# A local-attention stage with its first scores brought forward, its first softmax in halves, and a new order for the last tile

## The chip, the cores and the metric

The kernel runs on one core of one Trainium2 chip. The metric is device time in microseconds from the start to the end of the one program, taken as the median of several runs. All times in the profile are microseconds from the first instruction of one profiled execution.

## The reference

The reference is a small model of four residual layers on 4096 tokens (2 batches of 2048) of width 256: causal linear attention, a mixture of experts, local attention, and the same mixture of experts again. The change touches the third layer alone.

```python
windows = [max(4, 256 // 2**h) for h in range(16)]           # 256 128 64 32 16 8 4 4 ...
qk = layernorm(x) @ Wqk + bqk;  q, k = split(qk);  v = k
mask = (j <= i) & (j > i - windows[h])
att = softmax(where(mask, q @ k.T / 4, -inf));  out = att @ v  # 16 heads of 16
gates = softmax(layernorm(x) @ Wgate + bgate)                  # one per head
x = x + (out * gates) @ Wproj + bproj
# then, in the fourth layer
probs = softmax(layernorm(x) @ gate_w.T)                       # 8 experts
# threshold routing with a capacity per expert over all 4096 tokens, then two matmuls per expert
```

Six heads have windows of 256 down to 8; ten heads have a window of 4, and for them a token needs its own key and those of the three tokens before it.

## The kernel before

The 4096 tokens are 32 tiles of 128. Four tiles make a group (`GT = 4`), there are eight groups (`NG = 8`), four to a batch. Names of a group's tiles are 0 to 3.

The local-attention stage handles the two kinds of heads apart. The ten narrow heads are computed **by token**, with tokens on the partitions and without TensorE: `by_token` projects a tile on TensorE and VectorE adds the bias and puts the result into `tk` (L968); `shifts` copies the keys by one, two and three tokens into `ks` with small DMAs on SyncE's queue (L999 to L1004); `multiply` forms query times key (`pr`, L1044 and L1045); `sum_scores` sums over the 16 dimensions (`s4`, L1049); `softmax_begin` and `softmax_end` are the softmax over four scores, with the gate multiplied in; `weigh_values` multiplies the values (`pv`, on GpSimd, L1075 and L1078) and `sum_values` sums them (`og`, L1084). The six wide heads are computed **by channel**: `by_channel` projects a whole group with channels on the partitions (`qm`, `kT`); a `Tile` then does `scores` on TensorE, `maxima` on VectorE, `exponentials` on ScalarE, `transpose` (three PSUM tiles of 3, 4 and 2 blocks, for head 0, for heads 1 to 3, and for heads 4 and 5), `coefficients` (`cb`), `others` (the transposes `c_ps` of `og` and `cb`), `values` (`wo_ps`), and `project` (`pj_ps`, added to `x`). `Group.add_bias` adds the output bias to `x` on GpSimd (L955), `gates_begin` and `gates_end` are the gate's softmax, `values` builds the value tiles `wvm` and `wvb`.

When a tile's `x` is final, `finished` measures its mean and variance for the router. The router of a group, `Route`, does `normalize`, `transposes`, `logits`, `probabilities`, `normalized` (which writes `probs` and sends the rows to `rows_b` by DMA), `pairs` and `ranks` (which write `score`). The last group has two routes of two tiles each, `tails[0]` and `tails[1]`. After the last, the experts' first step reads all scores and loads its constants `cst_sel` by a DMA from GpSimd's queue.

The order of the instructions on TensorE, ScalarE, VectorE and GpSimd is written out by hand: inside `tc.manual_schedule(engines=ORDERED)` each engine issues in the order in which the program calls. SyncE's DMAs are placed by the scheduler. The opening brings group 0 up to its scores by token and group 1 up to its transposes; then `slot(g, i, now, last)` runs once for each tile, doing the second half of the tile before it (`last`), the first half of its own (`now`), and one quarter of the preparation of the next group (`coming`), of the norm of the one after (`behind`) and of the router of the one before (`past`). A tail of calls follows the last slot. The PSUM pool `mm` has four buffers, which all of these share. The opening and the loop before:

```python
own.transposes(None); own.keys_before()
for i in range(GT):
    own.by_token(i)
    if i % 2: own.shifts(i - 1, i + 1)
own.values()
for m in range(2): own.by_channel(m)
own.gates_begin(); own.gates_end(); own.add_bias()
measure(groups, 1, *range(GT)); then.norm.scale()
then.normalize(range(GT)); then.transposes()
for i in range(GT):
    own.multiply(i, nc.vector); own.sum_scores(i)
then.add_bias()
```

Of the kernel before, what the change touches and what calls it, by code (L numbers as in the profile page):

```python
# [16 lines left out]
P = 128  # L17
# [3 lines left out]
GT = 4  # L21
# [101 lines left out]
def hybrid_kernel(ctx: ExitStack, tc: tile.TileContext, x, wq, wk, wv, wo, wqk, bqk, wgate, bgate, wproj, bproj,  # L123
# [788 lines left out]
    def windowed_attention(src, added, route):  # L912
        src_t = src[0:N, :].rearrange("(g n p) d -> g p n d", p=P, n=GT)
        with ExitStack() as st:
# [22 lines left out]
            class Group:  # L937
# [84 lines left out]
                def gates_begin(self):  # L1022
                    self.gl = gl = pool.tile([P, GT, H], F32, name="gl", tag="gl")
                    gm = pool.tile([P, GT], F32, name="gm", tag="gm")
                    logits = self.tk[:, :, D4 + D : TOK]
                    nc.vector.reduce_max(gm, logits, axis=AX.X)
                    nc.vector.tensor_tensor(gl, logits, gm.unsqueeze(2).to_broadcast([P, GT, H]), ALU.subtract)
                    nc.scalar.activation(gl, gl, AF.Exp)

                def gates_end(self):  # L1030
                    gl = self.gl
                    gs = pool.tile([P, GT], F32, name="gs", tag="gs")
                    nc.vector.reduce_sum(gs, gl, axis=AX.X)
                    nc.vector.reciprocal(gs, gs)
                    nc.vector.tensor_tensor(gl, gl, gs.unsqueeze(2).to_broadcast([P, GT, H]), ALU.mult)
# [16 lines left out]
                def softmax_begin(self):  # L1052
                    s4 = self.s4
                    if self.first:
                        s4e = s4[:, 0, 1:NW, :].rearrange("p w h -> p (w h)")
                        nc.vector.tensor_tensor(s4e, s4e, con("shift"), ALU.add)
                    self.m4 = m4 = pool.tile([P, GT, NH4], F32, name="m4", tag="m4")
                    nc.vector.reduce_max(m4, s4.rearrange("p i w h -> p i h w"), axis=AX.X)
                    nc.vector.tensor_tensor(s4, s4, m4.unsqueeze(2).to_broadcast([P, GT, NW, NH4]), ALU.subtract)
                    nc.scalar.activation(s4, s4, AF.Exp, scale=0.25)  # L1060

                def softmax_end(self):

                    s4, m4 = self.s4, self.m4
                    nc.vector.reduce_sum(m4, s4.rearrange("p i w h -> p i h w"), axis=AX.X)
                    nc.vector.reciprocal(m4, m4)
                    nc.vector.tensor_tensor(m4, m4, self.gl[:, :, H4:H], ALU.mult)
                    nc.vector.tensor_tensor(s4, s4, m4.unsqueeze(2).to_broadcast([P, GT, NW, NH4]), ALU.mult)
                    self.og = pool.tile([P, GT, D4], F32, name="og", tag="og")
                    self.pvs = {}  # L1070

                def weigh_values(self, i):
                    s4 = self.s4
                    self.pvs[i] = pv = pool.tile([P, D4, NW], F32, name="pv4", tag="pr4", bufs=4)
                    nc.gpsimd.tensor_tensor(pv[:, :, 0].rearrange("p (h d) -> p h d", d=HD),  # L1075
                                            s4[:, i, 0, :].unsqueeze(2).to_broadcast([P, NH4, HD]),
                                            self.own[:, i, :].rearrange("p (h d) -> p h d", d=HD), ALU.mult)
                    nc.gpsimd.tensor_tensor(  # L1078
# [7 lines left out]
            class Tile:  # L1086


                def __init__(self, g, i):
                    self.g, self.i, self.t = g, i, (g % BG) * GT + i  # L1090

# [55 lines left out]
                def transpose(self, k):  # L1147
# [7 lines left out]
                    nc.scalar.copy(pt[:, skip:w, :], ps[:, skip:w, :])  # L1155
                    if k == 0:
                        self.pts = []
                    self.pts.append(pt)
# [79 lines left out]
            def slot(g, i, now, last):  # L1238
# [3 lines left out]
                if last:  # L1242
# [3 lines left out]
                    call(groups, last.g, "sum_values", last.i)  # L1246
                if i == 0 and g:
                    call(groups, g, "softmax_begin")
                if now:
# [4 lines left out]
                if now:  # L1254
                    now.maxima()
                    now.exponentials((2, 3))
                if i == 0 and not g:
                    now.exponentials((4, 5, 1, 0))
                    groups[0].softmax_begin()

                if i == 0:
                    call(groups, coming, "keys_before")
                    call(groups, g, "softmax_end")
# [10 lines left out]
                else:  # L1274
# [4 lines left out]
                    if g == NG - 1:  # L1279
# [153 lines left out]
```

## Time and profile before

| what | value |
|---|---|
| median of 3 runs | 940.69 us (940.29 to 940.84) |
| the profiled execution: its own time | 943.79 us |
| its span, first to last instruction | 941.7 us |
| mean granted TensorE clock | 0.906 |
| busy, share of the span | PE 80%, PE weight loads 53%, DVE 67%, ACT 40%, POOL 46% |
| 464.2 to 506.7 us, opening of local attention | PE 31.4, DVE 24.8, ACT 12.6, POOL 13.7 us busy of 42.5; clock 0.72 |
| 506.7 to 762.8 us, its tiles | PE 248.1, DVE 218.3, ACT 165.6, POOL 137.4 us busy of 256.1; clock 1.00 |
| 762.8 to 793.4 us, last tile and router | PE 16.1, DVE 19.7, ACT 8.3, POOL 5.4 us busy of 30.6; clock 0.75 |

In the profile PE is TensorE (PEld its weight loads), DVE VectorE, ACT ScalarE, POOL GpSimd, SPq the DMA queue that SyncE issues. A row gives the start, the duration, the engine, the line of the kernel, the operation, and output and input by the program's names; a bracket at the end gives how long the engine had been idle and what ended that. Idle time matters where its engine is the one that the rest waits for. The lines in the profile of before are those of the kernel before; in the changed kernel they stand a few lines lower.

### The profile page before, as it was taken

Reading aid. Unit: us, or ns where it says so; the run is one execution under the profiler, and the core shown is the slowest. Engines: PE = TensorE matmul, PEld = TensorE weight load, DVE = VectorE, ACT = ScalarE, POOL = GpSimd, SP = SyncE. Lnnn points to the kernel's source line nnn. Section 1 sums busy time; section 2 is a strip of 40 time slices with the busy share of each in tenths; the row PEclk is TensorE's granted clock in tenths of the full one; section 3 lists DMA queues with packets and bytes.
Section 4 is the critical chain, followed back from the end, with each engine's and each line's share of the span. In section 5 each row is a group of like instructions: output and inputs, shape, how many; then the busy total and the mean of one; then the engine's idle time right before and its main releaser. Section 6 shows DMA issues by size and latency. Waiting matters only on the chain. (4 is left out here: it accounts for less than half of the span.)

```text
span 941.7 us, 17226 instructions
## 1 busy us (share of the span) xinstructions
PE 755.1 (80%) x6422; PEld 494.6 (53%) x6422; DVE 627.8 (67%) x1670; ACT 380.3 (40%) x1075; POOL 436.7 (46%) x482
## 2 busy tenths in 40 slices
PE   6799999999998217877569999999999982168774
PEld 3576676676676114544335666665666661145442
DVE  4577778778677775532247878988988876755421
ACT  3444454544543122211124576675676661221110
POOL 2133334334234007888522644664655431058885
PEclk9799999999999557999778999999999995569997
DMA  9910101101102103455552123123132111025554
GB/s 317 264 36 24 47 2 47 47 2 47 46 20 74 31 0 81 76 83 83 111 152 59 41 58 95 33 81 94 30 89 84 57 46 41 1 70 74 80 81 60
DMA packets 64236, 65.08 MB, mean 69 GB/s; under 512 B 7084, under 2 KB 60825, under 8 KB 64153
## 3 DMA queue, kind: packets, MB, share of 16 engines
q1 hardware_dynamic: 50057, 44.00, 15.2%
q0 software_dynamic: 12720, 18.10, 11.8%
q10 hardware_dynamic: 1376, 1.90, 0.6%
q8 instruction: 50, 0.82, 0.4%
q14 instruction: 33, 0.27, 0.1%
HBM read 26.56 MB, written 27.56 MB: 57 GB/s over the span
## 5 line engine op out<-in xcount | busy, mean ns | idle before, releaser
L210 POOL TENSOR_TENSOR ln_rstd<-ln_rstd,cst_parts 128x4 f32<-128x4 f32 (+1 forms) x34 | 34.2, 1006 | 126.3 <-DVE ln_rstd L209 72.3
L235 ACT COPY xnT<-xnT_ps 128x512 f32<-128x512 f32 (+1 forms) x71 | 39.1, 579 | 127.0 <-PE xnT_ps L231 127.0
L883 PE MATMUL h_ps<-xnT,w_sb 128*128 128x512 f32 x128 | 67.8, 676 | 5.3 <-ACT xnT L235 3.5
L413 POOL TENSOR_TENSOR a_sb<-a_raw,cst_first 128x512 f32<-128x512 f32 x32 | 40.9, 1279 | 63.2 <-ACT a_raw L412 63.2
L896 DVE TENSOR_SCALAR y<-y_ps,xe 128x256 f32<-128x256 f32 x64 | 30.9, 484 | 51.8 <-PE y_ps L893 47.4
L893 PE MATMUL y_ps<-w_sb,hT 128*128 128x256 f32 x256 | 61.3, 386 | 4.6 <-DVE row L839 1.7
L415 DVE TENSOR_TENSOR a_sb<-s_ps,cst_first 128x512 f32<-128x512 f32 x96 | 60.0, 680 | 6.8 <-PE s_ps L401 6.8
L897 POOL DMA_INDIRECT out_rows<-y,idx x32 | 53.0, 1656 | 15.0 <-issue 7.3
L897 POOL DMA_INDIRECT mid<-y,idx x32 | 53.0, 1657 | 14.1 <-issue 7.9
L205 DVE BATCH_NORM_STATS2 ln_stats<-x 128x6 f32<-128x256 f32 x128 | 53.4, 418 | 8.5 <-DMA x<-in_x 4.4
L1155 ACT COPY pt<-pt_ps 128x256 f32<-128x256 f32 (+3 forms) x96 | 43.0, 469 | 38.8 <-PE pt_ps L1153 38.3
L966 PE MATMUL tk_ps<-wt_sb,xnT 128*128 128x432 f32 x128 | 56.2, 570 | 0.2 <-ACT xnT L235 0.2
L893 PEld LDWEIGHTS y_ps<-w_sb,hT 128*128 128x128 f32 x256 | 45.5, 189 | 18.2 <-ACT hT L885 3.9
L1144 ACT ACTIVATE wpr<-sn_ps,negm 128x128 f32<-128x128 f32 x128 | 45.9, 375 | 5.3 <-DVE negm L1130 5.3
L233 DVE COPY xnT<-xnT_ps 128x512 f32<-128x512 f32 (+1 forms) x29 | 19.0, 655 | 41.5 <-PE xnT_ps L231 41.4
L883 PEld LDWEIGHTS h_ps<-xnT,w_sb 128*128 128x128 f32 x128 | 26.2, 217 | 37.5 <-issue 25.8
L1153 PE MATMUL pt_ps<-cst_parts,wpr 128*128 128x128 f32 x280 | 44.0, 282 | 1.9 <-ACT wpr L1144 1.7
L1153 PEld LDWEIGHTS pt_ps<-cst_parts,wpr 128*128 128x128 f32 x280 | 30.8, 140 | 25.2 <-issue 6.9
L859 POOL DMA_INDIRECT xe<-rows_a,idx x32 | 33.7, 1054 | 20.9 <-DVE olo L812 11.7
L222 ACT ACTIVATE xr<-x,ln_shift,ln_rstd 128x256 f32<-128x256 f32 x56 | 29.1, 591 | 33.2 <-DVE ln_shift L220 18.6
L859 POOL DMA_INDIRECT xe<-rows_b,idx x32 | 32.7, 1023 | 20.9 <-DVE olo L812 11.4
L885 ACT ACTIVATE hT<-h_ps 128x512 f32<-128x512 f32 x32 | 19.1, 597 | 57.4 <-PE h_ps L883 56.2
(237 smaller groups left out, 2074.1 us busy)
## 6 DMA issues: line engine op xcount, KB each, us to landing
ks<-tk SPq DMA_DIRECT2D x21, 280.0 KB
rows_a<-xr SPq DMA_DIRECT2D x7, 528.0 KB
rows_b<-xr SPq DMA_DIRECT2D x7, 528.0 KB
x<-in_x SPq DMA_DIRECT2D x7, 512.0 KB
mid<-x SPq DMA_DIRECT2D x7, 512.0 KB
x<-mid SPq DMA_DIRECT2D x7, 512.0 KB
out_rows<-x SPq DMA_DIRECT2D x7, 512.0 KB
w_sb<-in_w1t SPq DMA_DIRECT2D x1, 2048.0 KB
```

What stands on the lines that cost most here:

```text
L205: nc.vector.bn_stats(self.stats[:, i, :], self.xin[:, i, :])
L235: nc.scalar.copy(xnT[:, c, :], pt)
L413: nc.gpsimd.tensor_tensor(a, raw, causal, ALU.mult)
L415: nc.vector.tensor_tensor(a, s_ps[j], causal, ALU.mult)
L859: read = nc.gpsimd.indirect_dma_start(out=xes[e][:, b, :], out_offset=None, in_=rows[:, :], in_offset=bass.IndirectOffsetOnAxis(ap=idx[e][ ...
L883: nc.tensor.matmul(h_ps, w1_sb[:, e, c, f * P : (f + 1) * P], xT[:, c, :], start=(c == 0), stop=(c == NC - 1))
L893: nc.tensor.matmul(y_ps, hT[:, f, b * P : (b + 1) * P], w2_sb[:, e, f, :], start=(f == 0), stop=(f == F // P - 1))
L897: add = nc.gpsimd.indirect_dma_start(out=acc[:, :], out_offset=bass.IndirectOffsetOnAxis(ap=idx[e][:, b : b + 1], axis=0), in_=y, in_offse ...
L966: nc.tensor.matmul(ps, self.xnT[:, c, i * P : (i + 1) * P], wt_sb[:, c, :], start=(c == 0), stop=(c == NC - 1))
L1144: nc.scalar.activation(self.pr[:, o : o + w], src, AF.Exp, bias=self.negm[:, h : h + 1], accum_out=self.den[:, h : h + 1])
L1153: nc.tensor.transpose(ps[:, n, :], self.pr[:, (o + n) * P : (o + n + 1) * P], ident)
L1155: nc.scalar.copy(pt[:, skip:w, :], ps[:, skip:w, :])
```

## The change

The opening and the end are put in another order, and several steps learn to work on part of a group or on another engine.

- `gates_begin`, `gates_end`, `softmax_begin` and `softmax_end` take a range of tiles. The opening calls each twice, for tiles 0 and 1 and for tiles 2 and 3; all later groups call them for four tiles as before.
- In the opening `by_channel` comes ahead of `by_token`; the first tile's `scores`, `maxima` and `exponentials` come in the midst of the `by_token` calls and no longer in `slot(0, 0)`; group 1 is measured, normalized and transposed earlier; `multiply` of tiles 1 and 3 goes from VectorE to GpSimd, `weigh_values` of tile 0 from GpSimd to VectorE. `add_bias` of group 0 comes after the products, `add_bias` of group 1 after `slot(0, 1)`.
- The last tile has no slot of its own. Its `sum_values` comes before its last exponentials; its three transposes run in the order of its heads' exponentials, (4, 5), (1, 2, 3), (0), the first two of them copied by VectorE; `tails[0]` is normalized and transposed after the last tile's `others`; both tiles of `tails[1]` are normalized on VectorE; the router of group 6 (`before`) does its last steps among these.

The built program has the same DMAs. On SyncE's queue the first group's 18 shift copies are issued in another order: the small ones (L1002) of each half first, which read the tile before, and then the six large ones (L999, L1000), where it had them in turn.

```diff
-                def gates_begin(self):
-                    self.gl = gl = pool.tile([P, GT, H], F32, name="gl", tag="gl")
+                def gates_begin(self, a=0, z=GT):
+                    if a == 0:
+                        self.gl = pool.tile([P, GT, H], F32, name="gl", tag="gl")
+                    gl, n = self.gl[:, a:z], z - a
...
-                def weigh_values(self, i):
+                def weigh_values(self, i, engine=nc.gpsimd):
...
-                def transpose(self, k):
+                def transpose(self, k, engine=None):
...
-                    nc.scalar.copy(pt[:, skip:w, :], ps[:, skip:w, :])
+                    (nc.vector.tensor_copy if engine else nc.scalar.copy)(pt[:, skip:w, :], ps[:, skip:w, :])
...
                 own.normalize((1, 3))
+                measure(groups, 1, 0, 1)
                 own.transposes(None)
                 own.keys_before()
-                for i in range(GT):
-                    own.by_token(i)
-                    if i % 2:
-                        own.shifts(i - 1, i + 1)
-                own.values()
+                measure(groups, 1, 2, 3)
+                then.norm.scale()
                 for m in range(2):
                     own.by_channel(m)
-                own.gates_begin()
-                own.gates_end()
+                for i in range(2):
+                    own.by_token(i)
+                own.shifts(0, 2)
+                first = Tile(0, 0)
+                first.scores()
+                then.normalize(range(GT))
+                own.by_token(2)
+                first.maxima()
+                first.exponentials((2, 3, 4, 5, 1, 0))
+                own.by_token(3)
+                own.shifts(2, GT)
+                own.gates_begin(0, 2)
+                own.values()
+                own.multiply(0, nc.vector)
+                own.multiply(1)
+                then.transposes()
+                own.sum_scores(0)
+                own.gates_end(0, 2)
+                own.sum_scores(1)
+                own.softmax_begin(0, 2)
+                own.gates_begin(2, GT)
+                own.multiply(3)
+                own.multiply(2, nc.vector)
+                own.softmax_end(0, 2)
+                own.weigh_values(0, nc.vector)
+                own.sum_scores(2)
+                own.sum_scores(3)
+                own.gates_end(2, GT)
+                own.softmax_begin(2, GT)
                 own.add_bias()
-                measure(groups, 1, *range(GT))
-                then.norm.scale()
-                then.normalize(range(GT))
-                then.transposes()
-                for i in range(GT):
-                    own.multiply(i, nc.vector)
-                    own.sum_scores(i)
-                then.add_bias()
+                own.softmax_end(2, GT)
...
+                        if g == 0 and i == 1:
+                            then.add_bias()
...
+                now, before, own = Tile(NG - 1, GT - 1), routes[NG - 2], groups[NG - 1]
                 last.transpose(0)
                 last.transpose(1)
                 last.coefficients()
-                groups[last.g].sum_values(last.i)
+                own.sum_values(last.i)
                 last.transpose(2)
+                now.scores()
                 last.others()
+                now.maxima()
+                now.exponentials((2, 3))
+                before.probabilities()
+                own.sum_values(now.i)
+                now.exponentials((4, 5, 1, 0))
+                last.values()
+                now.transpose(2, nc.vector)
+                now.transpose(1, nc.vector)
+                last.project()
+                now.transpose(0)
+                now.coefficients()
+                now.others()
+                finished(last.g, last.i)
+                tails[0].normalize()
+                tails[0].transposes()
+                now.values()
+                before.normalized()
+                now.project()
+                tails[0].logits()
+                finished(now.g, now.i)
+                before.pairs()
                 tails[0].probabilities()
-                last.values()
-                last.project()
-                finished(last.g, last.i)
+                tails[1].normalize()
+                tails[1].transposes()
                 tails[0].normalized()
-                tails[1].normalize((0,))
-                routes[NG - 2].ranks()
-                tails[1].transposes()
+                before.ranks()
+                tails[1].logits()
                 tails[0].pairs(nc.vector)
-                tails[1].logits()
                 tails[1].probabilities()
                 tails[0].ranks()
                 tails[1].normalized()
```

## The prediction

> **What bounds the kernel now.** I read the share of each engine by slice first, then the waits of the stretch that the diff touches, then each engine's instructions there in order of time. Over the span PE is busy 80%, but not in the two stretches that change: the 21st and 22nd slice of the page (471 to 518 us) and the 33rd and 34th. The opening runs from the first load at 464.2 us to 506.7 us, where the first tile's `c_ps` starts; the end runs from 762.8 us to 793.45 us, where the experts' first threshold matmul starts. What lies between is issued in the same order before and after.
>
> The opening, in the order of time of SyncE, GpSimd, VectorE and TensorE:
>
> ```profile
> 479.58 0.78 SPq L999 DMA_DIRECT2D ks<-tk  x1
> 493.08 0.77 SPq L1002 DMA_DIRECT2D ks<-tk  x1
> ...
> 492.67 2.44 POOL L955 TENSOR_TENSOR x<-x,bproj_sb 128x1024 f32<-128x1024 f32 x1 [2.43 <-ACT wa_xn L222]
> ...
> 492.24 0.65 DVE L1045 TENSOR_TENSOR pr<-tk,ks 128x480 f32<-128x480 f32 x1
> 493.67 1.63 DVE L1044 TENSOR_TENSOR pr<-tk 128x160 f32<-128x160 f32 x1
> 496.08 0.66 DVE L1045 TENSOR_TENSOR pr<-tk,ks 128x480 f32<-128x480 f32 x1 [0.79 <-DMA ks<-tk]
> 504.05 1.11 DVE L968 TENSOR_TENSOR tk<-tk_ps,bt_sb 128x432 f32<-128x432 f32 x2
> 505.72 0.82 DVE L1084 TENSOR_REDUCE og<-pv 128x160 f32<-128x640 f32 x1
> ...
> 506.69 0.30 PE L1173 MATMUL c_ps<-cst_parts,og 128*128 128x128 f32 x1 [1.33 <-DVE og L1084]
> ```
>
> Columns: start, duration, engine, line, operation; in brackets the idle time and what ended it. To be seen: SyncE issues 18 shift copies back to back, 479.58 to 493.85, 0.79 us each; the last one lands 3.0 us after its issue began, at 496.08, and VectorE has been waiting. From there VectorE never leaves the path: 496.08 to 504.05 is 7.97 us (the products and sums of tiles 2 and 3, three maxima, the softmax), then 2.5 us to the end of `og`, and PE waits for `og`. The opening is bound by a DMA queue, then by VectorE. PE is not.
>
> The row at 493.67 has a second lesson. The same line takes 0.32 us at 490.35. Here it ends at 495.30, just after GpSimd's bias sum ends at 495.11: a VectorE product of two SBUF tensors stood still while a GpSimd product held on.
>
> ```profile
> 486.00:488.00 2.00, 0.00 (x0) 0.00 (x0) 1.76 (x8) 0.07 (x1) 0.00 (x0) 0.96 0.17 47
> 488.00:490.00 2.00, 0.00 (x0) 0.00 (x0) 1.03 (x5) 0.00 (x0) 0.78 (x1) 0.50 0.31 82
> ...
> 498.00:500.00 2.00, 2.00 (x4) 0.85 (x3) 1.97 (x4) 0.12 (x1) 0.00 (x0) 0.50 0.11 26
> 500.00:502.00 2.00, 2.00 (x5) 0.98 (x4) 1.50 (x5) 2.00 (x11) 0.00 (x0) 0.63 0.00 0
> ```
>
> Two-microsecond stretches; the third number from the right is the granted PE clock. PE went idle at 485.2; the clock halved near 488 and came back near 501.5.
>
> The end:
>
> ```profile
> 778.07 0.43 DVE L1214 TENSOR_TENSOR x<-pj_ps,x 128x256 f32<-128x256 f32 x1 [1.64 <-PE pj_ps L1212]
> 784.52 0.17 DVE L648 TENSOR_REDUCE r_max<-l_ps 128x2 f32<-128x16 f32 x1
> 786.11 0.18 DVE L660 TENSOR_TENSOR probs<-r_exp,r_sum 128x16 f32<-128x16 f32 x1
> ...
> 789.94 0.67 POOL L134 DMA_DIRECT2D cst_sel<-in_consts  x1 [3.27 <-DMA rows_b<-xr_end]
> ...
> 793.45 0.16 PE L727 MATMUL t_ps<-n_in,cst_sel 128*128 128x3 bf16 x1 [3.97 <-issue]
> ```
>
> The last `probs` (786.29) goes by GpSimd and SyncE to `rows_b`; GpSimd loads `cst_sel` only when that has landed; PE needs `cst_sel`. These 7.16 us stay. The other branch, pairs and ranks to `score`, is ready at 791.6 and has 1.9 us to spare. So the end is worth what it moves the last `probs`.
>
> **Opening: the copies start later.** `by_channel` now stands ahead of `by_token` on PE: four matmuls, 3.6 us in the trace at full clock. PE starts at 474.0 either way with 2.7 us of half clock (474.6 to 477.3). 3.44 + 1.45 us of work plus 1.35 lost puts the first `tk_ps` at 480.25, `tk` tile 0 at 480.9, tile 1 at 482.35. Now the three small L1002 copies are issued first and need tile 0 alone, so SyncE starts at 481.0 instead of 479.58: 9 copies are three small ones (2.34 us, from 509.22) and three pairs of 1.60, 7.14 us; two such sets keep the queue full (tiles 2 and 3 are there at 486.0 and 488.1). The last issue begins at 494.4 and lands at 497.4, 1.3 us later than before. Six more DMAs (wvb and the next group's L1004) follow and end near 499.3; their reader comes after 508, so this costs nothing.
>
> **Opening: what stands behind the landing.** Tiles 0 and 1 are multiplied, summed and put through the first half of the softmax before 495.3, so VectorE waits 2.1 us. Behind it, on VectorE, from rows of before (half-size operations between the 128x40 and the 128x4 row): product of tile 2 0.68; sum, reciprocal and two products of the half softmax 0.40 + 0.30 + 0.20 + 0.25; `weigh_values(0)`, moved here from GpSimd (there 1.49), 0.24 + 0.68; two sums 1.50; gates 0.65; maximum and subtraction 0.65; ScalarE's exponential with its hop 0.35; second half softmax 1.15. Sum 7.05 against 7.97: the maxima (1.5) and two products (1.8) have gone into the wait, and the rest has grown by halves. Without more, the first `tk` evacuation would come at 504.45: 0.4 later than now.
>
> **Opening: GpSimd is no longer idle.** Before, GpSimd did nothing from 495.55 to 504.2. Now its queue holds, behind the same landing, the product of tile 3 (1.21), group 0's bias sum (2.40, which before ran unseen at 483.35), the `wkT` copy and `weigh_values(1)` (0.48 + 1.06). VectorE's product at 498.8 stands until tile 3's product ends (0.5); while it runs the bias sum queues, takes the port next and holds the following product 2.4; one piece of `weigh_values(1)` gets between the two products of `weigh_values(0)` (0.5). Together 3.4 us. The bounds: 0, if VectorE slips through each time, and 4.4, if the copy blocks too (the copy at 780.12 did not stretch L213). I take 3.4, since it is the mechanism of the row at 493.67. Then `tk` comes at 507.85; its 2.5 us to `og` gains 0.2 behind `weigh_values(2)`. **Opening +4.0.** The cover that is gone is ScalarE's and PE's: both are early and must wait for VectorE. `pt` of tile 0 stands behind the second exponential on ScalarE, so PE idles from about 497 to 507.
>
> **Opening: the clock.** That idle time is far longer than the one at 485.2, which halved the clock after some 2.7 us. In the trace of before PE is at full clock at 506.7; afterwards it will start the slot at half. The Trainium skill (TensorE: Matmul & The Clock Gate, What's actually happening) has full rate return after about 3.4 us of sustained activity. The row speaks otherwise: PE was busy from 491.2, and the clock returned near 501.5, 10 us on, with transposes and narrow scores first and dense matmuls only from 497.5. By the rule the slot loses half of 3.4, 1.7 us; by the whole row up to 5; counting only the dense matmuls as the row's warm-up, 3.8 us, half of which is 1.9. I take 1.9, bounds 0 and 5. It is on the path: in that slot PE runs without a gap from 506.69 to 512.3.
>
> **Opening: group 1's bias sum** moves from 492.67 (hidden) to GpSimd's queue behind the `wvm` copies of slot (0,1), ahead of `ln_rstd` for group 2, which has 5.6 us of slack there. It will lie where 512.2 to 514.6 is now; VectorE's L1164 at 513.70 falls into it and `og(1)`, for which PE already waits 0.2 us, comes 0.9 later. Bounds 0 and 0.9; taken 0.9.
>
> Moved without cost, with their cover: `measure(1)` (eight instructions, 2.2 us) into VectorE's wait for `xnT` and `tk` at 471.8 to 477.2 (its load ends 1.05 MB into the queue, and 1.29 MB had moved by 470); `normalize` of group 1, four on ScalarE, 482.5 to 484.6, ahead of the exponentials that need 486.7; its transposes on PE before 488; the first scores on PE 481.7 to 483.85; the `wvm` copies and memsets on GpSimd while it waits for the copies.
>
> **End.** PE's `pt(2)` now precedes the scores (0.22), yet ScalarE's exponentials are paced by the same maxima and end at 769.35 as now. `og(3)` runs under them at 767.1 instead of at 772.4 behind GpSimd's tie product. Two `pt` copies go to VectorE (0.42 + 0.69, which it has free at 768.6 to 770.2). `pj(2)` 770.2, `x` 770.7, `cb` 771.2, `c_ps(3)` 771.6, normalize of tail 0 (0.73) 772.5, its transposes 772.9, `wo(3)` (1.45) to 774.4, `cT` 774.85, `pj(3)` 775.6: `x` starts near 775.7, where it is 778.07 now, 2.4 earlier. But what follows has grown. The old order had 6.45 us from `x` to `r_max` of tail 1. The new one: 2.1 to `ln_rstd`; two L213 on VectorE (one was on ScalarE) 0.73, with 0.6 behind GpSimd's pair products; transposes and copy at half clock 1.5; then `probs` of tail 0 0.55, ranks 1.2, pairs 1.5 on VectorE before `r_max`, which all wait behind the `xnT` copy: 8.2. Gain 2.4 - 1.7 = **0.7**, bounds -0.5 and 2.4.
>
> One rule speaks against this part. VectorE's two pair comparisons will run beside GpSimd's `ln_rstd` power. In the row, L660 (two SBUF inputs) at 779.68 takes its usual 0.17 beside that power (779.46 to 780.17). The skill (SBUF — State Buffer, SBUF: two separate sides) has VectorE with two SBUF inputs and GpSimd exclude each other for a whole instruction: that would add 0.7 and leave no gain. The row decides: 0.
>
> **Sum.** 4.0 + 1.9 + 0.9 - 0.7 = +6.1 us. The profiled execution took 943.79 for a span of 941.7, so its span would become 947.8; its time lies 3.1 above the median of the runs, 940.69, and I carry the difference, not the level: 946.8.
>
> **Rivals.** B: the port gives way. VectorE arrives first at each turn and GpSimd waits instead, the clock warms at once: opening +0.4 to +1.5, end -0.7, about 941.2. For: a half-finished wait is won by VectorE in most rows (L1164 at 505.30 ends with GpSimd's instruction, not after the next). Against: the second product depends on the first, so GpSimd finds the port free between them.
>
> C, the other side: the end keeps its 2.4 us. It turns on whether `r_max` of tail 1 starts when PE's `l_ps` is there, or behind VectorE's pairs; if VectorE has done them by then, `probs` falls to 783.9. With the opening as in B at +0.4 and the clock warm, -2.0: 938.7. For: PE and ScalarE have long gaps there. Against: 3.25 us of VectorE work stands in the order between the copy and `r_max`. It decides below 785.9 for the last `probs`, with `og(0)` before 507.
>
> D: the clock stays at half through the first slots, +9 to +12: 951.
>
> **Numbers.** Likeliest, port and clock as summed: 0.65, own range 943.5 to 949.6. B 0.14, C 0.16, D 0.05. A measurement of this kernel tells about 0.2% from no change, 1.9 us here. C lies beyond it on the fast side, B within, the others beyond on the slow side: 0.16, 0.14, 0.70. The range reaches from between B and C, 939.5, to 949.6.
>
> **What would show it.** Right: the last L1000 issue near 494.4; VectorE's L1047 of tile 2 released by the DMA near 497.4; L1071 or L1072 stretched from 0.2 to over 2 us beside L955; `c_ps` of tile 0 near 510.7; PE clock 0.5 at 505 to 513; the last `x` sum 2.4 earlier relative to slot (7,3), the last `probs` only 0.7. Wrong: those products at their usual 0.2 to 0.3 us, `c_ps` before 507, or a clock of 1.0 there.

## The result and the profile after

The changed kernel takes 945.45 us (median of 7 runs, 943.90 to 947.51) against 940.78 for the kernel before on the same chip (7 runs, 939.46 to 942.88): a ratio of 1.0052, 95% interval 1.0037 to 1.0066. It is slower by 4.7 us, half a per cent. The profiled execution took 944.69 us for a span of 942.9.

The two profiled executions differ by only 1.2 us in span, so the comparison is made by stage. From the first load of the local attention to the experts' first threshold matmul it is 462.87 to 796.49 after, 333.62 us, and 464.24 to 793.45 before, 329.21: **+4.41**. What lies ahead of it (1.37 less) and behind it (146.41 against 148.25) has the same instructions in both and is scatter of single executions: the profiled execution of before was a slow one, 3.1 us above the median of its runs, that of after 0.8 below. All times of after have to be read with 1.37 added when they are held against before.

The timeline of after, in its opening, in the order SyncE, GpSimd, VectorE, TensorE (start, duration, engine, line, operation; in brackets the idle time and what ended it):

```profile
479.90 2.18 SPq L1002 DMA_DIRECT2D ks<-tk  x3
...
493.54 0.85 SPq L1000 DMA_DIRECT2D ks<-tk  x1
...
495.82 1.68 POOL L1047 TENSOR_TENSOR pr<-tk,ks 128x480 f32<-128x480 f32 x1 [5.05 <-DMA ks<-tk]
497.47 2.33 POOL L955 TENSOR_TENSOR x<-x,bproj_sb 128x1024 f32<-128x1024 f32 x1
...
495.79 0.66 DVE L1047 TENSOR_TENSOR pr<-tk,ks 128x480 f32<-128x480 f32 x1 [2.04 <-DMA ks<-tk]
496.99 0.55 DVE L1071 TENSOR_TENSOR m<-m,gl 128x20 f32<-128x20 f32 x1
497.57 2.33 DVE L1072 TENSOR_TENSOR s<-s,m 128x80 f32<-128x80 f32 x1
499.93 0.51 DVE L1080 TENSOR_TENSOR pv<-s,tk 128x160 f32<-128x160 f32 x1
500.30 1.22 DVE L1083 TENSOR_TENSOR pv<-s,ks 128x480 f32<-128x480 f32 x1
...
505.06 0.24 DVE L1072 TENSOR_TENSOR s<-s,m 128x80 f32<-128x80 f32 x1
505.21 1.11 DVE L968 TENSOR_TENSOR tk<-tk_ps,bt_sb 128x432 f32<-128x432 f32 x2
...
507.79 0.45 PE L1177 MATMUL c_ps<-cst_parts,og 128*128 128x128 f32 x1 [2.72 <-DVE og L1089]
508.24 3.09 PE L966 MATMUL tk_ps<-wt_sb,xnT 128*128 128x432 f32 x4
```

To be seen: the first copies are issued at 479.90, 17.03 us behind the first load (15.34 before), the last one at 493.54, and VectorE's product of tile 2 is released by the copies at 495.79. GpSimd takes its own product 0.03 us later, then the bias sum at 497.47. VectorE's product L1072, of 80 elements, starts at 497.57 and ends at 499.90, just behind the bias sum at 499.80: 2.33 us, where the same line takes 0.24 at 505.06. `c_ps` comes at 507.79, and the first slot's `tk_ps` takes 3.09 us: TensorE is at half clock. The same row in the timeline of before, at full clock:

```profile
506.94 1.62 PE L966 MATMUL tk_ps<-wt_sb,xnT 128*128 128x432 f32 x4
```

Two half-microsecond stretches of after show where the clock changes (third number from the right):

```profile
499.50:500.00 0.50, 0.00 (x0) 0.00 (x0) 0.47 (x2) 0.00 (x0) 0.50 (x2) 0.82 0.04 9
513.00:513.50 0.50, 0.50 (x2) 0.13 (x1) 0.04 (x1) 0.00 (x0) 0.00 (x0) 0.53 0.02 4
```

A mean of 0.82 between 1.0 and 0.5 puts the fall at 499.82; 0.53 puts the return at 513.47, 5.7 us behind `c_ps`.

The timeline of after at its end, VectorE, GpSimd and TensorE:

```profile
779.93 0.42 DVE L1218 TENSOR_TENSOR x<-pj_ps,x 128x256 f32<-128x256 f32 x1 [0.26 <-PE pj_ps L1216]
781.14 0.42 DVE L671 TENSOR_TENSOR bef<-probs 128x256 f32<-128x256 f32 x1
782.15 1.52 DVE L213 TENSOR_SCALAR xr_end<-x,ln_mv,ln_rstd 128x256 f32<-128x256 f32 x2
788.08 0.17 DVE L648 TENSOR_REDUCE r_max<-l_ps 128x2 f32<-128x16 f32 x1
789.66 0.18 DVE L660 TENSOR_TENSOR probs<-r_exp,r_sum 128x16 f32<-128x16 f32 x1
...
781.31 0.80 POOL L210 TENSOR_TENSOR ln_rstd<-ln_rstd,cst_parts 128x2 f32<-128x2 f32 x1 [1.32 <-DVE ln_rstd L209]
782.09 0.63 POOL L673 TENSOR_TENSOR tie<-tie,cst_parts 128x256 f32<-128x256 f32 x1
793.04 0.67 POOL L134 DMA_DIRECT2D cst_sel<-in_consts  x1 [2.83 <-DMA rows_b<-xr_end]
...
796.49 0.17 PE L727 MATMUL t_ps<-n_in,cst_sel 128*128 128x3 bf16 x1 [3.46 <-issue]
```

Held against the first `pt` of slot (7, 3), which is at 767.33 after and 762.83 before, the last `x` comes 12.60 us behind it (15.24 before), the last `probs` 22.33 (23.28), the threshold matmul 29.16 (30.62). `x` to `r_max` has grown from 6.45 to 8.15 us.

### The profile page after: what moved, and what is told of

Same layout as the page of the kernel before. It is cut to its first block, busy times and chain, and to the rows that moved or that the text cites. A ratio compares the mean times of both kernels' runs of the same rounds, so it can differ in the third digit from the quotient of the medians.

```text
span 942.9 us, 17246 instructions
## 1 busy us (share of the span) xinstructions
PE 753.2 (80%) x6422; PEld 494.4 (52%) x6422; DVE 631.7 (67%) x1681; ACT 378.6 (40%) x1074; POOL 439.3 (47%) x484
```

## The experiments

Twelve kernels, in three groups of four. The kernel before had a median of 941.1 us on the chip of the first group, 942.87 on the second's and 939.62 on the third's, so kernels of different groups are compared by their ratio to it. The ratio and its interval are the record's, taken over all runs; the quotient of two medians differs from it by up to a thousandth, 0.9 us. The segments are of one execution each, and that one can lie several microseconds from the median of its kernel. Four segments of the stage can be cut out of every trace, all in us. "Landing" is the time from the first load of the stage to VectorE's product of tile 2, "VectorE" the time from there to the first `tk` evacuation of the slot, "slot" that from the first `c_ps` to the second, "end" that from the last `x` sum to the threshold matmul.

| kernel | ratio (95%) | landing | VectorE | slot | end |
|---|---|---|---|---|---|
| before | 1 | 31.84 | 7.97 | 8.15 | 15.38 |
| after | 1.0052 (1.0037 to 1.0066) | 32.92 | 9.42 | 11.52 | 16.56 |
| own_bias_early | 1.0034 (1.0019 to 1.0048) | 33.49 | 7.38 | 10.71 | 16.25 |
| both_bias_early | 1.0005 (0.9996 to 1.0015) | 33.80 | 7.38 | 10.52 | 16.55 |
| warm_gap | 1.0055 (1.0039 to 1.0071) | 31.82 | 9.46 | 8.82 | 16.72 |
| new_end_alone | 0.9996 (0.9984 to 1.0009) | 31.92 | 7.96 | 8.20 | 17.05 |
| both_and_warm | 1.0007 (0.9994 to 1.0020) | 32.36 | 7.40 | 8.18 | 16.56 |
| shifts_first | 0.9991 (0.9981 to 1.0001) | 30.89 | 7.39 | 9.88 | 16.63 |
| shifts_first_warm | 0.9969 (0.9959 to 0.9979) | 29.53 | 7.41 | 8.13 | 16.23 |
| end_rmax_first | 0.9973 (0.9961 to 0.9985) | 31.29 | 7.97 | 9.79 | 15.63 |
| gap_filled | 1.0031 (1.0015 to 1.0047) | 30.80 | 9.46 | 8.86 | 16.58 |
| both_gap_filled | 0.9997 (0.9983 to 1.0011) | 30.58 | 7.41 | 9.83 | 16.22 |
| best_no_fill | 0.9986 (0.9972 to 1.0001) | 28.95 | 7.38 | 10.88 | 15.53 |
| best | 0.9968 (0.9952 to 0.9983) | 30.80 | 7.42 | 9.83 | 15.26 |

VectorE's column repeats to 0.1 us wherever the order is the same. The end does so only to 0.8: 16.22 to 17.05 in the ten kernels with the changed order, 15.26 to 15.63 in the three with the order of end_rmax_first. Landing and slot vary most, and most of that is the clock, below.

**The bias sum of group 0 (own_bias_early).**

```diff
                 own.keys_before()
+                own.add_bias()
                 measure(groups, 1, 2, 3)
...
                 own.softmax_begin(2, GT)
-                own.add_bias()
                 own.softmax_end(2, GT)
```

> The changed kernel with one call moved: group 0's bias sum on GpSimd (L955, 2.33 us) goes from behind the products to the place right after keys_before, where GpSimd is idle. Theory (port exclusion): the softmax product L1072 of tiles 0 and 1, 2.33 us in the changed kernel, returns to 0.24, the first c_ps comes 1.5 to 2.1 us earlier relative to the stage's first load (44.9 us behind it now), and the time falls by 1.5 to 2.1 from 945.45, to about 943.6. Rival 1: the product was stretched by something else (its own operands, the DMA writes of the next group's copies at 496 to 498): L1072 stays above 2 us and the time stays at 945.4. Rival 2: the exclusion is only passed on, since GpSimd's next products (L1047 of tile 3, weigh_values of tile 1) now hold VectorE instead: L1072 or L1083 grows by about as much, and less than 0.8 us is gained.

Measured: 944.61 us, ratio 1.0034. The timeline of own_bias_early, VectorE's product and the bias sum in its new place:

```profile
498.07 0.36 DVE L1072 TENSOR_TENSOR s<-s,m 128x80 f32<-128x80 f32 x1
471.47 2.35 POOL L955 TENSOR_TENSOR x<-x,bproj_sb 128x1024 f32<-128x1024 f32 x1 [1.82 <-PE xnT_ps L231]
```

The product falls from 2.33 to 0.36 and VectorE's stretch from 9.42 to 7.38 us, 2.04 less. The copies of the next group ran at the same time as before, so the first rival is out; so is the second, since L1083 keeps its 1.22. The first `c_ps` moved by 1.5 only, because the landing was 0.6 later in this execution. The ratio fell by 1.8 thousandths, 1.7 us; taken alone that is not clear of noise, since its interval overlaps that of the changed kernel.

**Both bias sums (both_bias_early).** As above, and:

```diff
                 then.normalize(range(GT))
+                then.add_bias()
...
-                        if g == 0 and i == 1:
-                            then.add_bias()
```

> As own_bias_early, and group 1's bias sum (L955, 2.35 us beside slot (0, 1) in the changed kernel) also goes ahead, right behind group 1's normalize, where GpSimd is idle from 483.6 to 486.9 us. Theory: cb of tile 1 (L1168), 0.93 us there, returns to about 0.26, and the stretch from the pt of tile 1 to its c_ps falls from 3.94 to about 3.26 us: 0.7 less than own_bias_early, so about 2.5 us below the changed kernel, 942.9. Rival: og of tile 1 waits for its values on GpSimd or for PE anyway, and the 0.7 comes back as a wait: the same as own_bias_early.

Measured: 942.08 us, ratio 1.0005. The timeline of both_bias_early:

```profile
517.35 0.26 DVE L1168 TENSOR_TENSOR cb<-cf,gl 128x96 f32<-128x96 f32 x1
```

The same row in the timeline of after:

```profile
517.50 0.93 DVE L1168 TENSOR_TENSOR cb<-cf,gl 128x96 f32<-128x96 f32 x1
```

`cb` of tile 1 is back from 0.93 to 0.26. That this is worth its 0.7 us is seen in the slots that are at full clock: 8.82 and 8.86 with the bias sum (warm_gap, gap_filled), 8.13 and 8.18 without (shifts_first_warm, both_and_warm). In the medians the two bias sums make 4.7 thousandths of the time, 4.4 us, where the traces have 2.7. The two intervals do not meet, so the gain itself is clear of noise; its size is not, they allow about 2.8 to 6.1.

**TensorE kept busy ahead of the transposes (warm_gap, both_and_warm).** 34 matmuls, or 20 on top of both_bias_early:

```diff
+                if g == 0 and i == 1:
+                    warm(sc, groups[0].xnT[:, 0, :], 34, "sb")
                 if last:
                     last.transpose(0)
                     last.transpose(1)
```

> The changed kernel with 34 extra matmuls of 128x256 on TensorE, about 8.7 us, whose results nobody reads, put ahead of the first tile's transposes, where TensorE is idle for 8.5 us. Theory (cold clock): TensorE's clock stays at 1.0 until 508, the first slot's two tk_ps take 1.6 us instead of 3.1, the way from the first c_ps to the second tile's pt falls from 7.58 to about 4.9 us, and the time falls by 2 to 2.7 us, to about 943. Rival 1: the first slot is bound by other engines (the tk evacuations on VectorE, the pj_ps copy), so that a fast clock only makes TensorE wait: under 0.7 us gained. Rival 2: the matmuls push the transposes and scores late, c_ps starts after 508.5 relative to the changed kernel's 507.8, and half or more of the gain is lost.

> both_bias_early (942.08 us; its stage, from the first load to the experts' first threshold matmul, 331.4 us) with 20 extra matmuls of 128x256 on TensorE, about 8.3 us at the 0.42 us each took in warm_gap, ahead of the first tile's transposes; their results are not read. warm_gap shortened the stage of its trace by 2.8 us, yet its median was 945.81, so the cold clock's price in the time is open. Theory (cold clock is on the path): clock 1.0 through the first slot, no late c_ps this time, the way from the first c_ps to the third falls from 18.96 to about 16.6 us, the stage to about 329.0, and the time to about 939.7. Rival 1 (something outside the stage pays the extra matmuls back, as warm_gap's median says): the stage is shorter and the time stays at 942 or above. Rival 2: the stage does not shorten, since the clock comes back of itself within 2 us: 942.

Measured: 945.81 us (1.0055) and 942.56 us (1.0007): no gain in either. Yet the clock stayed at 1.0 and the slot was at 8.82 and 8.18. The timeline of warm_gap shows one reason:

```profile
492.69 14.19 PE L242 MATMUL warm_ps<-xnT 128*128 128x256 f32 x65
506.72 0.60 PE L1159 MATMUL pt_ps<-cst_parts,wpr 128*128 128x128 f32 x4
...
509.39 0.27 PE L1177 MATMUL c_ps<-cst_parts,og 128*128 128x128 f32 x1
```

A matmul of f32 counts as two in these rows: the 34 of the fill are 68, of which this view, which begins in the midst of them, has 65. So the four of `pj_ps` in 1.03 us, from which I had counted 0.26 us for a matmul, are two matmuls, and one takes 0.43 there and in the fill alike. The fill took 14.8 us, not 8.7. It runs over the end of the gap, the transposes and the scores come behind it, and `c_ps` starts with no wait at all: TensorE has become the late one, by 0.9 us. In both_and_warm, with 20 of them, `c_ps` waits 0.42 us for `og`: hardly any slack. So the fill can make `c_ps` late by whatever the phase of the clock takes from TensorE in the execution at hand. That this is all of the missing gain is not shown. The two traces also flatter: the profiled execution was the fastest of its kernel's in both, 2.1 and 2.2 us below the median.

**The same fill where only pt(2) stands behind it (gap_filled, both_gap_filled).**

```diff
                 if not begun:
                     now.scores()
+                if g == 0 and i == 1:
+                    for _ in range(20):
+                        nc.tensor.matmul(now.sbank[:, 256:512], groups[0].xnT[:, 0, 0:P], groups[0].xnT[:, 0, 0:256], ...)
                 if last:
                     last.transpose(2)
```

> The changed kernel with 20 extra matmuls of 128x256 on TensorE (8.4 us at 0.42 each) in the idle time itself, between the second tile's scores and the pt(2) of the first, so that only pt(2) stands behind them; they write the unused half of the bank of sb_ps and nobody reads them. In warm_gap 34 of them stood ahead of the transposes and made c_ps late, in both_and_warm 20 left no slack. Theory (a window of about 3.4 us in which TensorE idles halves the clock, and a whole window of dense work gives it back, so the first slot runs at half for 3.4 to 6.8 us): clock 1.0 at the first c_ps, from the first to the second c_ps about 8.9 us instead of 11.5, and the time 2.6 us below the changed kernel, a ratio of about 1.0025 to the kernel before. Rival (the fill is paid back elsewhere, as the medians of warm_gap and both_and_warm have it): the slot is shorter in the trace and the ratio stays near 1.005.

> both_bias_early with the same fill of 20 matmuls in the gap. Theory: the first slot 10.5 to about 8.2 us, ratio to the kernel before from 1.0005 to about 0.998. Rival (paid back elsewhere): ratio 1.0005 or above.

Measured: 942.86 us (1.0031) and 939.66 us (0.9997). The timeline of gap_filled:

```profile
494.65 8.90 PE L1259 MATMUL sb_ps<-xnT 128*128 128x256 f32 x40
503.39 0.38 PE L1160 MATMUL pt_ps<-cst_parts,wpr 128*128 128x128 f32 x2
506.29 0.30 PE L1178 MATMUL c_ps<-cst_parts,og 128*128 128x128 f32 x1 [2.52 <-DVE og L1089]
```

Now `c_ps` waits for `og` again, the slot is 8.86 us (8.9 was expected), and the ratio is 2.1 thousandths below the changed kernel's, 2.0 us of the 2.6 expected; the two intervals overlap. In the trace of both_gap_filled the clock fell all the same, at 504.28, just as `c_ps` began; its slot is 9.83, and its ratio gains 0.8 thousandths only:

```profile
504.27 0.45 PE L1178 MATMUL c_ps<-cst_parts,og 128*128 128x128 f32 x1 [2.16 <-DVE og L1089]
```

TensorE was idle there for 2.16 us, in gap_filled for longer, 2.52. What differs is where the idle time lay. The clock changes of each trace stand 3.41 us, or a multiple of it, apart (see the end of this document). On the grid of both_gap_filled the idle time lies inside one stretch, 500.86 to 504.28, of which TensorE was busy 37%; on that of gap_filled it lies across 504.72, and the two stretches were busy 72% and 54%. That would explain it, but the share of busy time alone is no rule: a stretch that was busy 61% kept the clock in before (504.89 to 508.30) and lost it in end_rmax_first (503.26 to 506.67). So the same fill holds the clock in one execution and can lose it in another.

**The shift copies first (shifts_first, shifts_first_warm).** On top of both_bias_early:

```diff
-                for m in range(2):
-                    own.by_channel(m)
-                for i in range(2):
-                    own.by_token(i)
-                own.shifts(0, 2)
-                first = Tile(0, 0)
-                first.scores()
                 then.normalize(range(GT))
...
+                for i in range(GT):
+                    own.by_token(i)
+                    if i % 2:
+                        own.shifts(i - 1, i + 1)
+                for m in range(2):
+                    own.by_channel(m)
                 then.add_bias()
+                first = Tile(0, 0)
+                first.scores()
```

> both_bias_early with by_token of all four tiles and their shift copies ahead of by_channel and of the first scores, as the kernel before had them; group 1's normalize goes ahead of them too. Theory (the last shift copy's landing sets when the products start): the first tk is there about 2 us earlier, VectorE's product of tile 2 is released by the copies at about 31.8 us behind the stage's first load instead of 33.8, the first c_ps at about 41.8 instead of 43.75, and the time is about 2 us below both_bias_early, 940.1. Rival 1: VectorE, which has the maxima and the products of tiles 0 and 1 to do, is the later of the two, and the copies wait for nobody: under 0.7 us gained. Rival 2: TensorE's first scores and ScalarE's exponentials come so late that they, or the transposes of group 1 behind them, now set the end: no gain or a loss.

> shifts_first with 15 extra matmuls (about 6.3 us) on TensorE ahead of the first tile's transposes, results not read. Theory (landing, port and clock add up): stage about 327 us, 2.2 below the kernel before, time about 937.7, a ratio of 0.9965. Rival: the extra matmuls are paid back outside the stage: as shifts_first or above.

Measured: 941.55 us (0.9991), and 939.73 us (0.9969) with 15 matmuls ahead of the transposes. The timeline of shifts_first:

```profile
493.52 0.77 SPq L1002 DMA_DIRECT2D ks<-tk  x1
495.57 0.66 DVE L1047 TENSOR_TENSOR pr<-tk,ks 128x480 f32<-128x480 f32 x1 [1.58 <-DMA ks<-tk]
```

VectorE still waits 1.58 us for the last copy, so the queue and not VectorE sets the start; the landing is at 30.89 instead of 33.80 and the first `c_ps` at 40.86 instead of 43.75. (33.80 was a late one; see the part on the copies below.) In the time, shifts_first gains 1.4 thousandths over both_bias_early, 1.3 us of the 2 expected, and the two intervals overlap. shifts_first and shifts_first_warm ran on the same chip, and their intervals do not meet: the fill is worth 1.8 us there, with the slot at 8.13 instead of 9.88. It is the one pair in which the fill's gain is clear of noise.

**The end alone, and its last step (new_end_alone, end_rmax_first).** new_end_alone is the opening and first slots of the kernel before with the end of the changed one. end_rmax_first adds:

```diff
                 tails[1].logits()
-                tails[0].pairs(nc.vector)
                 tails[1].probabilities()
+                tails[1].normalized()
+                tails[0].pairs(nc.vector)
                 tails[0].ranks()
-                tails[1].normalized()
```

> The kernel before with the new end alone: opening and first slots as before, the last tile and the router's tails in the order of the change. Theory (the two parts add up, the opening costs and the end gains): the way from the pt of slot (7, 3) to the experts' first threshold matmul is about 29.2 us instead of 30.6, and the time is 0.7 to 1.5 us below the kernel before, 939.3 to 940.1, a ratio of 0.9985 to 0.9993. Rival 1: the end gains nothing by itself and the 1.46 us between the two profiles are scatter of the DMAs around rows_b and cst_sel: ratio 1.000. Rival 2: the end loses, and the opening cost less than the trace says: ratio above 1.001.

> new_end_alone with one change in VectorE's order at the very end: r_max, r_exp and probs of the last two tiles stand ahead of the pair comparisons and ranks of the two before (probs of the two routes get a buffer each). Theory (the end's gain was eaten by VectorE work ahead of r_max): x to r_max of the last route falls from 8.14 to about 6.9 us, the last probs comes 1.2 to 1.4 us earlier (4.72 us behind its r_max-less x now 9.7), and since the scores then end 0.5 later, the first threshold matmul comes 0.8 to 1.3 earlier: stage about 327.2 instead of 328.3, time 939.4 to 939.9. Rival 1: the last score, which moves later, becomes the late branch: the threshold matmul does not move, 940.7. Rival 2: r_max waits for l_ps from TensorE anyway: probs moves under 0.4 us.

(The 4.72 in the second text is a slip; the comparison meant is with the 9.72 us from the last `x` to the last `probs`.) Measured: 940.71 us (0.9996, interval 0.9984 to 1.0009) and 940.57 us (0.9973). For the end alone the trace gives 29.65 us from the `pt` of slot (7, 3) to the threshold matmul, 1.0 less than before; the median shows 0.4 and cannot tell that from nothing. The timeline of end_rmax_first:

```profile
784.48 0.17 DVE L660 TENSOR_TENSOR probs<-r_exp,r_sum 128x16 f32<-128x16 f32 x1
...
788.09 0.67 POOL L134 DMA_DIRECT2D cst_sel<-in_consts  x1 [3.17 <-DMA rows_b<-xr_end]
...
792.21 0.16 PE L727 MATMUL t_ps<-n_in,cst_sel 128*128 128x3 bf16 x1 [2.15 <-DVE hit L724]
```

From the last `x` it is 7.90 us to the last `probs` (9.72), and 15.63 to the threshold matmul (17.05), with new_end_alone's in brackets: 1.8 and 1.4 less. (17.05 is the longest of the ten ends with the changed order; against the middle of the ten, 16.56, it is 0.9.) The matmul's bracket has changed from "issue", its load of `cst_sel`, to VectorE's `hit`: the branch of the scores is now the late one, and takes 0.4 of the 1.8 back.

**Together (best_no_fill, best).** shifts_first with the order of end_rmax_first, without and with 10 matmuls in the gap.

> The same as best without the extra matmuls: shifts_first and the order of end_rmax_first. Theory: 1.5 to 2 us below shifts_first, a ratio of 0.997 to the kernel before; and 2 us above best, which is the price of the cold clock. Rival: the end's gain (0.9973 for end_rmax_first against 0.9996 for new_end_alone) was scatter of the chips: ratio 0.999.

> All that helped in one kernel: shifts_first, with 10 extra matmuls in the gap ahead of pt(2) (4.2 us; the gap there is about 6), and VectorE's order of end_rmax_first. Theory (they add up): shifts_first 0.9991, less 2 us for the clock and 1.5 to 2 for the end, gives a ratio of 0.995 to the kernel before, about 4.5 us. Rival: the clock's part is not there in the time: 0.997.

Measured, on one chip: 939.35 us (0.9986) and 937.36 us (0.9968). best is 2.3 us faster than the kernel before by the medians, 3.0 by the ratio, and so beats both kernels. It missed its 0.995: in its trace the clock fell just as `c_ps` began (slot 9.83), behind 2.52 us of idle time that the 10 matmuls had left. shifts_first_warm, with 15, has the same ratio without the gain at the end.

best_no_fill missed too. Its 0.9986 is the rival's 0.999 rather than the theory's 0.997, and no more than half a thousandth below shifts_first, so the gain of the end's order, which end_rmax_first showed with 0.9973, did not come again on top of shifts_first. The intervals are too wide to say which of the two is the exception; the traces have the shorter end in all three kernels. best against best_no_fill, the price of the clock, is 1.8 thousandths with intervals that overlap. And end_rmax_first, shifts_first_warm and best cannot be told from each other, though they have different parts of the gains.

## Why the prediction was right

It said 946.8 us, slower, +6.1; measured are +4.7 in the medians and +4.41 in the traces of the stage. Each mechanism it named is there in the trace; several of its sizes were off, in both directions. By its own steps:

- **The copies start later:** +1.3 predicted, 1.08 in the pair of traces, but by two errors that partly cancel. The first copy is issued 1.69 later behind the first load (17.03 against 15.34) where 1.4 was taken: in the trace of before the clock was at half from 474.17 to 477.58, 3.41 us, and the prediction had read 2.7. On the other hand the last copy releases its reader 2.25 us after its issue began, where the 3.0 of before had been carried over. That time goes with the order: 3.00 to 3.17 in three traces of the old opening, 2.25 or 2.26 in all seven of the new one, 2.04 to 2.06 in the four of shifts_first's; why, stays open.

  The order causes the late start. In the seven executions whose clock fell 9.3 to 10.2 us behind the first load and came back 3.4 later, the first copy is at 16.80 to 17.17 with the new order and at 15.24 to 15.39 with `by_token` first; where the clock did not fall it is 15.02 to 15.51 against 13.40 and 13.61.

  The size of the landing depends on the execution. With the new order it was between 30.58 and 33.80 us, the latest in both_bias_early, whose clock was at half until 14.7 us behind the first load, the earliest in gap_filled and both_gap_filled, without a fall there. Not all of it is the clock: warm_gap has no fall either and 31.82, because its copies took 14.06 us from first to last issue instead of 13.3.
- **VectorE behind the landing:** 7.05 of bare work predicted, and 3.4 of waiting for the port, +2.5. Measured +1.45. The waiting was right: L1071, L1072, L1080 and L1083 take 0.55, 2.33, 0.51 and 1.22 where products of these sizes take 0.18, 0.24, 0.32 and 0.65 elsewhere, 3.2 together; own_bias_early takes 2.04 of it away by moving one instruction. The bare work is the term that was mis-sized: 9.42 less 3.2 is 6.2, not 7.05. I had put operations on half the tiles midway between larger and smaller rows (0.40 for a sum over 80, which takes 0.28), and I had added durations, although the next row mostly begins some 0.1 us before the end of one: the two sums of 1.52 take 1.44 from start to start, the product of 0.66 takes 0.57. So this stretch would have been 0.6 shorter than before if the bias sum had stayed hidden: 7.38 against 7.97, as the eight kernels show that have it moved.
- **The clock:** +1.9 predicted, between 0 and 5. In the pair of traces the slot grew by 3.37, of which the bias sum is 0.68: 2.7. The return was taken from the row of before (its 3.8 us of dense matmuls are 4.0, from 497.50 to 501.47), and the rule beside it I read too short. The Trainium skill (TensorE: Matmul & The Clock Gate, What's actually happening) has the activity watched in windows of 3413 ns that run freely, whenever the work starts. My estimate from this figure: work which starts inside a window stays at half until the end of the next, 3.4 to 6.8 us at half clock, a loss of 1.7 to 3.4. The traces agree. In after the clock changes at 499.82 and 513.47, 13.65 us apart, four times 3.41, and the 5.7 us at half behind `c_ps` make 2.8 of loss, for the 2.7 measured. In all eight traces whose clock is down in the first slot it is so for 3.4 to 5.8 us of it, and the slot is 1.6 to 2.7 us longer than at full clock, a little under half of that time each. One value was the wrong kind of answer; the range held it.
- **Group 1's bias sum:** +0.9 predicted, 0.7 measured.
- **The end:** -0.7 predicted, between -0.5 and 2.4 of gain. The last `x` came 2.64 earlier (2.4), `x` to `r_max` grew to 8.15 (8.2), the last `probs` came 0.95 earlier (0.7). The threshold matmul moved by 1.46; the other 0.5 lies between `probs` and that matmul, 6.83 us in all after and 7.34 before, in DMAs that the change does not touch; new_end_alone, with the new order, has 7.33 there, so this half microsecond is scatter and not a gain of the change. The mechanism, VectorE work in front of `r_max`, is what end_rmax_first removes.
- **The rule not taken** was rightly left: the two pair comparisons, at 781.14 and behind, take 0.42 each, the second wholly beside GpSimd's power for `ln_rstd` (781.31 to 782.11). The stretch came with the next instruction: two L213 take 1.52 instead of 0.73, beside GpSimd's tie product, which the prediction had at 0.6.

Rival B, the port that gives way, is refuted by L1072 in after and by own_bias_early. Rival C needed `r_max` ahead of VectorE's pairs; it is what end_rmax_first builds, not what the change did. Rival D did not come: the clock is back in the second slot in every trace.

The sum was 1.4 above the median. Against the traces, 0.85 of bare VectorE work, 0.8 at the end and 0.9 of smaller terms (the landing, the port, the way from `tk` to `og`, group 1's bias sum) were put too slow, and 0.8 of the clock too fast; the median lies 0.3 above the traces. So the number came closer than its terms deserved. Luck had a part in it: in the traces of the five kernels that leave the gap unfilled the loss to the clock is 1.7 to 2.7 us, by the phase of the execution, and 0.5 of the end's gain in the pair was scatter.

What stays open: warm_gap and both_and_warm are 2.8 and 4.2 us shorter in the stage of their trace than the kernels they were built on, and no faster in the median. Part of this is which executions are compared: both were profiled in their fastest execution, and both_bias_early in its slowest of 21, 3.2 us above its median. No run separates the rest from another cause.

## What to carry to other kernels

An instruction that ran unseen on an idle engine is not free where it is moved to: ask which port, queue or clock it shares at the new place. When an opening is bound by a queue of small copies, put first what fills the queue, and let the other engines' early work go behind it. Idle time of TensorE on the way to a dense stretch costs twice, once as the wait and once as the clock behind it; a fill helps only if nothing that others wait for stands behind it, and the idle time that it leaves can still cost the clock, by the phase of the execution.

## What the runs showed of the hardware

The granted clock changes on a grid. In after it rises or falls at 469.1, 472.5, 475.9, 489.6, 493.0, 499.8 and 513.5, in before at 487.82 and 501.47: all multiples of 3.41 us apart within one execution, and at another phase in each. The same opening as before got a slot of 8.15 and 8.20 us in two executions and 9.79 in a third (end_rmax_first), so the kernel before pays for the cold clock too, now and then. That can be a part of the 2 to 7 us that lie between the fastest and the slowest run of a kernel; how large a part is not shown.

Being busy is not enough for the return. In before PE is busy with hardly a gap from 491.2 to 501.5. Two whole windows of it (stretches of 3.41 us on the grid), up to 498.06, held mostly transposes and narrow scores and left the clock at half; the third, with dense matmuls, gave it back. In after one window of dense projections, 489.6 to 493.0, was enough. The two other traces with the opening of before show the same: the clock stays at half over a stretch of transposes and scores without a gap (493.22 to 496.63 in new_end_alone, 493.02 to 496.43 in end_rmax_first). Why such a stretch does not count, the traces do not tell.

Of two products, one on VectorE and one on GpSimd, the one that starts later waits, in three rows of after. A product of 80 elements on VectorE waits 2.1 us for one GpSimd product of 1024 elements that began 0.1 us before it (497.57 and 497.47). At 488.73 VectorE's product of 480 elements takes 1.66 instead of 0.66, behind a GpSimd product of the same size that began at 488.68. At 495.79 VectorE is 0.03 us ahead and keeps its 0.66, and there GpSimd's product takes 1.68 instead of 1.2.
